# A graph-attention layer's softmax sums: half of head 0's in every fourth tile to GpSimd, transfers and copies in other places

## The chip, the cores and the metric

The kernel runs on one core of a Trainium2 chip. A core has five engines that run side by side, each with its own queue of instructions in a fixed order: TensorE (PE in the profile; PEld is its weight loads) multiplies matrices, VectorE (DVE) and ScalarE (ACT) work elementwise, GpSimd (POOL) does so more slowly and also issues DMA transfers, and SyncE (SP) issues transfers. Engines wait for one another by semaphores. The metric is the device time of one execution in microseconds (us); the time before is 2834.48 us, the median of three runs (2832.46 to 2835.08).

## The reference, cut to what matters

The model has two layers over a graph of 4096 nodes with 512 features. Layer 0 is a masked dot-product attention; the change doesn't touch it. Layer 1 is a graph attention with 8 heads of 64 columns:

```python
h = relu(layernorm(x))
data1 = (h @ W.T + b).reshape(N, H, D)              # N 4096, H 8, D 64
src = einsum('nhd,xhd->nh', data1, src_proj)        # one number per node and head
trg = einsum('nhd,xhd->nh', data1, trg_proj)
e = src.T[:, :, None] + trg.T[:, None, :]           # (head, n, m)
e = where(e >= 0, e, 0.01 * e)
e = e + adj[None, :, :]                             # added to the logit, not a mask
out = einsum('hnm,hmd->hnd', softmax(e, axis=-1), data1.transpose(1, 0, 2))
x = x + out.transpose(1, 0, 2).reshape(N, H * D)
```

For every head there are 4096 x 4096 weights, of which each output needs a weighted sum over m and the plain sum of the weights (the softmax's denominator).

## The kernel before, in words

Layer 1 works in *groups* (`groups`): 4 blocks of 1024 output nodes n (`WL`) by 2 halves of 4 heads (`HG`), so 8 groups, and in each group over 32 *tiles* of 128 neighbours m (`NT`). A step is one tile of one group. The weights of a tile lie with m on the partitions and n along the row, 128 x 1024 in fp32, one tile `pr0` to `pr3` for each head.

The exponential of the leaky logit is a product of row and column factors. ScalarE computes `ex`, the exponential of the adjacency tile (`exps`, line 1071, into PSUM, a single buffer), and `e3`, the same with a column factor (`last_exps`, line 1081, into SBUF). VectorE makes each head's weights in one instruction (`weigh`): max of a row factor `z` and a column factor, times `ex` (line 1122, heads 1 and 2) or times `e3` (line 1122, head 3, whose inputs both lie in SBUF); head 0 takes its maximum from a relu on ScalarE (`relus`, line 1104, tile `rl`, two buffers) and only subtracts and multiplies (line 1119). The order on VectorE is heads 3, 0, 1, 2. In the eight tiles of `BY_LOG` (3, 7, ..., 31) head 0's weights come from ScalarE instead: a relu `lg` of a row `u` (`logs`, line 1087), to which GpSimd adds the adjacency in two halves (`add_logs`, line 1093), and an exponential into `pr0` (line 1101). `pr0` has three buffers, `pr1` to `pr3` have two.

TensorE (`gather`) multiplies the tile's 128 neighbours' values by the weights: 16 matmuls of 32 columns by 512 (line 1157), which run four at a time in four column strips of the array, into the accumulators `pv` in PSUM. The denominators are accumulated in the bank `dn`. For heads 1 and 2 a further matmul per half row does it (line 1162). Head 3's weights are summed over the tiles on GpSimd (`acc3`, line 1133, 128 x 1024). Head 0's are summed by transfers: GpSimd issues a DMA that adds `pr0` to one of two accumulators in SBUF, in turn (line 1140), in the 24 tiles of `BY_DMA`, and TensorE sums the other eight (6, 10, 14, 18, 22, 26, 29, 31) with a column of ones, in whichever half of the strips is named by `side`. At a group's last tile TensorE adds the accumulators themselves.

The schedule is by hand. In step s the list `stages` calls each function for a tile some steps ahead: adjacency load 4 (SP), `exps` and `weigh` 1, `factors` (`e3` and relu) 2, `logs` 4, `gather` 0. Each engine gets its instructions in this order; so in step 9 VectorE makes tile 10 and GpSimd sums it, while TensorE multiplies tile 9. At a group's last tile four copies on ScalarE (line 1190) free `pv`; the copy of `dn` (line 1196) stands in the next step, behind the next relu. The group's results are finished during the next group (`finish`), one piece in each of the 15 steps of `PARTS`: transposes on TensorE, four scalings on ScalarE (line 1243) in two steps in a row, and behind the second a transfer on GpSimd that adds the layer's input to the output block `o` (line 1248, in steps 5, 9, 13 and 17); SP stores `o` three steps later (line 1246), the last one in step 18 (line 1251). In groups 0 and 1 ScalarE also scales two value blocks per tile (line 1067).

Of the kernel before, what the change touches and what calls it, by code (L numbers as in the profile page):

```python
# [8 lines left out]
FP = mybir.dt.float32  # L9
AF = mybir.ActivationFunctionType  # L10
ALU = mybir.AluOpType
# [4 lines left out]
P = 128  # L16
# [12 lines left out]
def kernel(  # L29
# [57 lines left out]
    ones = big.tile([P, 1], FP, name="ones")  # L87
# [5 lines left out]
    rl = s_n.rearrange("p h t -> p (h t)").rearrange("p (t b) -> p t b", b=NB)  # L93
# [9 lines left out]
    with tc.tile_pool(name="w0", bufs=1) as wp, tc.tile_pool(name="a0", bufs=2) as ap_, tc.tile_pool(  # L103
        name="a0s", bufs=8
# [259 lines left out]
        for b in range(1, NB):  # L364
            n = 0
# [120 lines left out]
    with tc.tile_pool(name="mx", bufs=1) as mxp, tc.tile_pool(name="b_a", bufs=6) as adjp, tc.tile_pool(  # L486
        name="b_m", bufs=4
    ) as mkp, tc.tile_pool(name="b_s", bufs=2) as sp, tc.tile_pool(
        name="b_p", bufs=6, space=PSUM
# [53 lines left out]
        early = {}  # L543
# [35 lines left out]
        for n in range(-5, len(items)):  # L579
# [3 lines left out]
            if n >= 0:  # L583
                i, j, t = items[n]
# [10 lines left out]
                if n in more:  # L595
                    f, m = more[n]
# [7 lines left out]
    with tc.tile_pool(name="c_e", bufs=4) as etp, tc.tile_pool(name="c_a", bufs=4) as adjp, tc.tile_pool(  # L604
        name="c_d", bufs=2
    ) as wkp, tc.tile_pool(name="c_m", bufs=1) as mxp, tc.tile_pool(name="c_o", bufs=4) as iop, tc.tile_pool(
        name="c_s", bufs=2
# [9 lines left out]
        src, aj, ex, mbs = {}, {}, {}, {}  # L617
# [104 lines left out]
        left, scale, norms, zs = [], {}, iter(()), {}  # L722
# [177 lines left out]
        for s in range(-5, end):  # L900
            n, q = divmod(s, NQ)
# [50 lines left out]
    va = sup.rearrange("p t (h d) -> p t h d", h=H)  # L952
# [30 lines left out]

    PARTS = (0, 1, 2, 4, 5, 6, 8, 9, 10, 12, 13, 14, 16, 17, 18)
    BY_LOG = (3, 7, 11, 15, 19, 23, 27, 31)
    BY_DMA = [m for m in range(NT) if m not in (6, 10, 14, 18, 22, 26, 29, 31)]
    after = mybir.DependencyInfo(mybir.DependencyClass.Sync, mybir.DependencyReason.DATA)

    with tc.tile_pool(name="p", bufs=2) as prp, tc.tile_pool(name="rl", bufs=2) as rlp, tc.tile_pool(
        name="io1", bufs=2
    ) as iop, tc.tile_pool(name="s1", bufs=1) as sp, tc.tile_pool(name="za", bufs=1) as zp0, tc.tile_pool(name="e3", bufs=2) as e3p, tc.tile_pool(
        name="zb", bufs=1
# [86 lines left out]
            nc.scalar.activation(x_, ra[i, m], AF.Exp, bias=ld_m[:, h // HG, m:m + 1])  # L1081
            e3[i, m] = x_

        def logs(i, m):
            if m in BY_LOG:
                r = rlp.tile([P, WL], FP, name="lg", bufs=1)
                nc.scalar.activation(r, us[i], AF.Relu, bias=nlg_m[:, groups[i][1], m:m + 1], scale=-(1.0 - SLOPE))
                rl[i, m] = r

        def add_logs(i, m, half, behind=None):  # L1090
            if m in BY_LOG:
# [15 lines left out]
        def weigh(i, m, order=ORDER):  # L1107
            h = groups[i][1] * HG
            x_ = ex.pop((i, m))
            for k in order:  # L1110
                if (i, m, k) in pr:
                    continue
                w = prp.tile([P, WL], FP, name=f"pr{k}", bufs=3 if k == 0 else 2)
                if k == 0 and (i, m) == (0, 0):
                    r = rlp.tile([P, WL], FP, name="rl")
                    nc.vector.tensor_scalar(r, zs_[0, 0], g_m[:, 0, 0:1], d_m[:, 0, 0:1], ALU.max, ALU.mult)
                    nc.vector.tensor_tensor(w, r, x_, ALU.mult)
                elif k == 0:
                    nc.vector.scalar_tensor_tensor(w, rl.pop((i, m)), ngd_m[:, h // HG, m:m + 1], x_,  # L1119
                                                   op0=ALU.subtract, op1=ALU.mult)  # L1120
                else:
                    p_ = nc.vector.scalar_tensor_tensor(w, zs_[i, k], g_m[:, h + k, m:m + 1],  # L1122
                                                        e3.pop((i, m)) if k == 3 else x_,
                                                        op0=ALU.max, op1=ALU.mult)
                    if k == 3:
                        add_logs(i, m + 1, 1, p_)
                pr[i, m, k] = w
            w = pr[i, m, 3]
            if m == 1:
                acc[i, 3] = acp.tile([P, WL], FP, name="acc3", bufs=1)  # L1130
                nc.gpsimd.tensor_tensor(acc[i, 3], pr[i, 0, 3], w, ALU.add)
            elif m > 1:
                nc.gpsimd.tensor_tensor(acc[i, 3], acc[i, 3], w, ALU.add)  # L1133
            add_logs(i, m + 2, 0)
            if m == 1:
                for n in range(2):
                    acc[i, 0, n] = acp.tile([P, WL], FP, name=f"acc0{n}", bufs=1)
                    nc.gpsimd.dma_start(acc[i, 0, n], pr[i, n, 0])
            elif m > 1 and m in BY_DMA:
                nc.gpsimd.dma_start(acc[i, 0, (len(BY_DMA) + BY_DMA.index(m)) % 2], pr[i, m, 0], accum_op=ALU.add)  # L1140

        def gather(i, m):
            b, g = groups[i]
            last = m == NT - 1
            if m == 0:
                pv[i] = ([[p_v.tile([P, BL], FP, name=f"pv{c}{q}") for q in range(HV)] for c in range(2)],
                         p_v.tile([P, BL], FP, name="dn"))
            v, dn = pv[i]
            by_pe = [u for u in range(NT) if u not in BY_DMA]
            side = sum(u < m for u in by_pe) % 2  # L1150

            def values(c):
                for q in range(HV):
                    for r in (side, 1 - side):
                        k = ((3, 0), (1, 2))[c][r]
                        for c0 in range(0, D, Q):
                            nc.tensor.matmul(v[c][q][r * D + c0:r * D + c0 + Q, :],  # L1157
                                             va[:, m, g * HG + k, c0:c0 + Q],
                                             pr[i, m, k][:, q * BL:(q + 1) * BL], start=(m == 0), stop=last)

            def den(r, w, src, q, **fl):
                nc.tensor.matmul(dn[r * Q:r * Q + w.shape[1], :], w, src[:, q * BL:(q + 1) * BL], **fl)  # L1162

            values(0)
            if last:
                for r, a in enumerate((acc[i, 0, 0], acc[i, 3])):
                    for q in range(HV):
                        den(r * HV + q, zo[:, 1:3], a, q, start=False, stop=False)
                if m in by_pe:
                    for q in range(HV):  # L1170
                        den(side * HV + q, zo[:, 1 - side:3], pr[i, m, 0], q, start=False, stop=False)
            values(1)
            for r in (side, 1 - side):
                for q in range(HV):
                    hk = g * 2 + r
                    den(r * HV + q, d0_m[:, hk, m, :] if m else d0_0[:, hk, :], pr[i, m, r + 1], q,
                        start=(m == 0), stop=(last and r == 1))
            if m in by_pe and not last:
                for q in range(HV):
                    den(side * HV + q, zo[:, 1 - side:3], pr[i, m, 0], q, start=False, stop=False)  # L1180
            if last:
                for q in range(HV):
                    den(q, zo[:, 1:3], acc[i, 0, 1], q, start=False, stop=True)
            for k in range(HG):
                pr.pop((i, m - 1, k), None)
            if last:
                os_ = [[osp.tile([P, BL], FP, name=f"os{c}{q}") for q in range(HV)] for c in range(2)]
                for c in range(2):
                    for q in range(HV):
                        nc.scalar.copy(os_[c][q], v[c][q])  # L1190
                late[i] = os_, dn

        def denominators(i):
            os_, dn = late.pop(i)
            od = osp.tile([P, BL], FP, name="od")
            nc.scalar.copy(od, dn)
            yield os_
# [56 lines left out]
        def finish_last(i):  # L1254

            ys = [ep.tile([P, WT // 2, HG, D], FP, name="e") for _ in range(2)]
            for n in range(2):
                nc.sync.dma_start(ys[n], part(x1, i, n * WT // 2, WT // 2))
            yield
            dens = denominators(i)  # L1260
            os_ = next(dens)
            pts = []
# [67 lines left out]
        weigh(0, 0, (3, 1, 2, 0))  # L1330
        scale(0, 0)
        factors(0, 1)
        logs(0, 3)
        scale(0, 1)

        stages = ((load, 4), (exps, 1), (weigh, 1), (factors, 2), (logs, 4), (scale, 2), (gather, 0))
        for s in range(len(steps)):
            for f, ahead in stages:
                if s + ahead < len(steps):
# [47 lines left out]
```

## Time and profile before

| | |
|---|---|
| profiled execution | 2832.0 us (span 2829.9) |
| median of three runs | 2834.48 us |
| TensorE busy | 2760.9 us, 98% of the span |
| VectorE busy | 2506.6 us, 89% |
| ScalarE, GpSimd busy | 1474.1 us (52%), 1395.4 us (49%) |
| layer 1, groups 1 to 7 | about 148 us each: VectorE 144 to 148, TensorE 147 to 149, GpSimd 117 to 121 |
| granted TensorE clock | 0.991 over the execution |

A line of a group of instructions names the source line, the engine, the operation, the tile written and the tiles read, the shape, the count, then the busy time in us and the mean of one in ns, then the engine's idle time just before these instructions and what ended it. A line of the timeline has the start and length in us, and in brackets the idle time before. Instructions of one engine overlap a little: the next may start shortly before the recorded end of the one before.

### The profile page before, as it was taken

Reading aid. Unit: us, or ns where it says so; the run is one execution under the profiler, and the core shown is the slowest. Engines: PE = TensorE matmul, PEld = TensorE weight load, DVE = VectorE, ACT = ScalarE, POOL = GpSimd, SP = SyncE. Lnnn points to the kernel's source line nnn. Section 1 sums busy time; section 2 is a strip of 40 time slices with the busy share of each in tenths; the row PEclk is TensorE's granted clock in tenths of the full one; section 3 lists DMA queues with packets and bytes.
Section 4 is the critical chain, followed back from the end, with each engine's and each line's share of the span. In section 5 each row is a group of like instructions: output and inputs, shape, how many; then the busy total and the mean of one; then the engine's idle time right before and its main releaser. Section 6 shows DMA issues by size and latency. Waiting matters only on the chain. (4 is left out here: it accounts for less than half of the span.)

```text
span 2829.9 us, 46835 instructions
## 1 busy us (share of the span) xinstructions
PE 2760.9 (98%) x16843; PEld 1488.1 (53%) x16843; DVE 2506.6 (89%) x3425; ACT 1474.1 (52%) x2217; POOL 1395.4 (49%) x1182
## 2 busy tenths in 40 slices
PE   7999999999999999999999799999999999999998
PEld 4885444445888888888885323323222322232222
DVE  7877799898987788888886699999999999999998
ACT  2212233333133333433432188988788878888786
POOL 5323434444010010011106687887878787878786
PEclk9999999999999999999999999999999999999999
DMA  5536898887899999998866379999999898989896
GB/s 173 175 103 254 274 338 294 298 292 268 185 188 213 194 222 256 226 219 238 221 194 158 109 195 240 241 213 249 218 246 222 239 223 237 227 242 218 211 224 168
DMA packets 535992, 629.86 MB, mean 223 GB/s; under 512 B 292152, under 2 KB 346456, under 8 KB 535760
## 3 DMA queue, kind: packets, MB, share of 16 engines
q1 hardware_dynamic: 461920, 415.87, 49.2%
q0 software_dynamic: 71824, 207.07, 33.5%
q10 hardware_dynamic: 2016, 3.93, 0.4%
q8 instruction: 132, 2.16, 0.3%
q14 instruction: 100, 0.82, 0.1%
HBM read 404.23 MB, written 107.15 MB: 181 GB/s over the span
## 5 line engine op out<-in xcount | busy, mean ns | idle before, releaser
L1157 PE MATMUL pv<-pr,sup 128*32 128x512 f32 x8192 | 986.6, 594 | 18.0 <-POOL sup L1065 14.9
L1133 POOL TENSOR_TENSOR acc<-acc,pr 128x1024 f32<-128x1024 f32 x240 | 575.0, 2396 | 149.6 <-DVE pr L1122 148.0
L1122 DVE SCALAR_TENSOR_TENSOR pr<-z,g_m,ex 128x1024 f32<-128x1024 f32 x512 | 630.4, 1270 | 4.4 <-ACT ex L1071 2.6
L1157 PEld LDWEIGHTS pv<-pr,sup 128*32 128x32 f32 x8192 | 280.2, 110 | 618.9 <-issue 563.8
L525 PE MATMUL pe<-he_t,he_t 128*128 128x512 f32 x896 | 387.9, 594 | 0.0
L679 ACT ACTIVATE d<-d 128x1024 f32<-128x1024 f32 x126 | 133.1, 1056 | 441.4 <-DVE d L671 216.9
L1122 DVE SCALAR_TENSOR_TENSOR pr<-z,g_m,e 128x1024 f32<-128x1024 f32 x256 | 343.8, 1343 | 3.4 <-PE pv L1157 3.2
L1071 ACT ACTIVATE ex<-e 128x1024 f32<-128x1024 f32 x256 | 263.2, 1028 | 144.7 <-DVE pr L1122 142.9
L1162 PE MATMUL dn<-pr,d_m 128*2 128x512 f32 x1984 | 318.1, 592 | 0.0
L1081 ACT ACTIVATE e<-e,ld_m 128x1024 f32<-128x1024 f32 x256 | 290.8, 1136 | 0.0
L525 PEld LDWEIGHTS pe<-he_t,he_t 128*128 128x128 f32 x896 | 169.9, 191 | 209.3 <-issue 193.7
L717 PE MATMUL po<-sup,u 128*128 128x256 f32 x1024 | 263.7, 380 | 0.0
L717 PE MATMUL po<-he_t,at 128*128 128x256 f32 x1024 | 262.9, 379 | 0.0
L717 PE MATMUL po<-sup,at 128*128 128x256 f32 x1024 | 245.1, 382 | 8.9 <-DVE at L688 7.7
L1119 DVE SCALAR_TENSOR_TENSOR pr<-rl,ngd_m,ex 128x1024 f32<-128x1024 f32 x191 | 242.6, 1270 | 8.4 <-ACT ex L1071 8.4
L1104 ACT ACTIVATE rl<-z,ngd_m,d_m 128x1024 f32<-128x1024 f32 x191 | 234.7, 1229 | 0.0
L804 POOL DMA_DIRECT2D he_t<-he_t x56 | 48.8, 949 | 356.5 <-ACT he_t L720 302.1
L688 DVE TENSOR_TENSOR at<-d,a 128x1024 f32<-128x1024 f32 x126 | 154.1, 1223 | 71.7 <-PE po L717 47.0
L717 PEld LDWEIGHTS po<-sup,at 128*128 128x128 f32 x1024 | 194.9, 191 | 39.0 <-DVE at L688 11.5
L717 PEld LDWEIGHTS po<-he_t,at 128*128 128x128 f32 x1024 | 194.5, 190 | 26.7 <-issue 0.3
L717 PEld LDWEIGHTS po<-sup,u 128*128 128x128 f32 x1024 | 194.4, 190 | 26.3
L530 POOL DMA_DIRECT2D er_d<-mk x136 | 74.5, 548 | 239.1 <-DVE rm L527 226.7
(271 smaller groups left out, 3830.8 us busy)
## 6 DMA issues: line engine op xcount, KB each, us to landing
e<-in_adj_t_dram SPq DMA_DIRECT2D x256, 512.0 KB, 5.9
acc<-pr POOLq DMA_DIRECT2D x192, 512.0 KB, 6.1
a<-in_adj_t_dram SPq DMA_DIRECT2D x126, 512.0 KB, 5.3
ac<-in_adj_t_dram SPq DMA_DIRECT2D x124, 256.0 KB, 5.2
ar<-in_adj_dram SPq DMA_DIRECT2D x120, 256.0 KB, 4.8
ec_d<-mc POOLq DMA_DIRECT2D x120, 256.0 KB, 4.9
er_d<-mk POOLq DMA_DIRECT2D x112, 256.0 KB, 4.6
et<-er_d SPq DMA_DIRECT2D x448, 64.0 KB, 4.1
```

Source lines behind the costliest of these rows:

```text
L525: nc.tensor.matmul(pe[:, :w], he_t[i][:, k, (t % TB) * P:(t % TB + 1) * P], he_t[j][:, k, BL - w:], start=(k == 0), stop=(k == KC - 1))
L679: nc.scalar.activation(d, d, AF.Exp)
L688: nc.vector.tensor_tensor(w, d, aj.pop((n, q)), ALU.mult)
L717: nc.tensor.matmul(acc[:, j, :], A[:, j * P:(j + 1) * P], B, start=(first_ and j == 0), stop=last, skip_group_check=True)
L1071: nc.scalar.activation(x_, ra.pop((i, m)), AF.Exp)
L1081: nc.scalar.activation(x_, ra[i, m], AF.Exp, bias=ld_m[:, h // HG, m:m + 1])
L1104: nc.scalar.activation(r, zs_[i, 0], AF.Relu, bias=ngd_m[:, h // HG, m:m + 1], scale=d_m[:, h, m:m + 1])
L1119: nc.vector.scalar_tensor_tensor(w, rl.pop((i, m)), ngd_m[:, h // HG, m:m + 1], x_, op0=ALU.subtract, op1=ALU.mult)
L1122: p_ = nc.vector.scalar_tensor_tensor(w, zs_[i, k], g_m[:, h + k, m:m + 1], e3.pop((i, m)) if k == 3 else x_, op0=ALU.max, op1=ALU.mult)
L1133: nc.gpsimd.tensor_tensor(acc[i, 3], acc[i, 3], w, ALU.add)
L1157: nc.tensor.matmul(v[c][q][r * D + c0:r * D + c0 + Q, :], va[:, m, g * HG + k, c0:c0 + Q], pr[i, m, k][:, q * BL:(q + 1) * BL], start=(m = ...
L1162: nc.tensor.matmul(dn[r * Q:r * Q + w.shape[1], :], w, src[:, q * BL:(q + 1) * BL], **fl)
```

## The change

- Head 0's sums: the tiles without a transfer are now 4, 8, ..., 28 (`BY_HALF`) and 31. In each of the seven, GpSimd copies or adds one half row (512 columns) of `pr0` into a new accumulator `acc02`, the halves taking turns, and TensorE sums the other half with one matmul; at the last tile TensorE sums `pr0` of tile 31 and `acc02`. The 24 transfers are those of all other tiles, so tiles 6, 10, 14, 18, 22, 26 and 29 have one now.
- The strips in `gather` start at one of four places, by the number of half matmuls so far, in place of one of two.
- At a group's end only the first two copies of `pv` stand behind the last tile. The other two, and the copy of `dn`, come behind the next group's exponential of tile 1 (`rest`, `copy_rest`).
- The log relu of tile 3 is made one step earlier (`early_logs`, 5 ahead), so in step 30 of the group before, in which VectorE makes tile 31.
- The relu's tile `rl` has one buffer in place of two.
- The last piece of `finish`, the last store, moves from step 18 to 21.

```diff
-    PARTS = (0, 1, 2, 4, 5, 6, 8, 9, 10, 12, 13, 14, 16, 17, 18)
+    PARTS = (0, 1, 2, 4, 5, 6, 8, 9, 10, 12, 13, 14, 16, 17, 21)
     BY_LOG = (3, 7, 11, 15, 19, 23, 27, 31)
-    BY_DMA = [m for m in range(NT) if m not in (6, 10, 14, 18, 22, 26, 29, 31)]
+    BY_HALF = (4, 8, 12, 16, 20, 24, 28)
+    BY_DMA = [m for m in range(NT - 1) if m not in BY_HALF]
...
-    with tc.tile_pool(name="p", bufs=2) as prp, tc.tile_pool(name="rl", bufs=2) as rlp, tc.tile_pool(
+    with tc.tile_pool(name="p", bufs=2) as prp, tc.tile_pool(name="rl", bufs=1) as rlp, tc.tile_pool(
...
-        def logs(i, m):
-            if m in BY_LOG:
+        def logs(i, m, early=False):
+            if m in BY_LOG and early == (m == BY_LOG[0]):
                 r = rlp.tile([P, WL], FP, name="lg", bufs=1)
                 nc.scalar.activation(r, us[i], AF.Relu, bias=nlg_m[:, groups[i][1], m:m + 1], scale=-(1.0 - SLOPE))
                 rl[i, m] = r
+
+        def early_logs(i, m):
+            logs(i, m, True)
...
             elif m > 1 and m in BY_DMA:
                 nc.gpsimd.dma_start(acc[i, 0, (len(BY_DMA) + BY_DMA.index(m)) % 2], pr[i, m, 0], accum_op=ALU.add)
+            if m in BY_HALF:
+                n = BY_HALF.index(m)
+                if n == 0:
+                    acc[i, 0, 2] = acp.tile([P, WL], FP, name="acc02", bufs=1)
+                a, w = (t[:, (1 - n % 2) * BL:(2 - n % 2) * BL] for t in (acc[i, 0, 2], pr[i, m, 0]))
+                if n < 2:
+                    nc.gpsimd.tensor_copy(a, w)
+                else:
+                    nc.gpsimd.tensor_tensor(a, a, w, ALU.add)
...
-            by_pe = [u for u in range(NT) if u not in BY_DMA]
-            side = sum(u < m for u in by_pe) % 2
+            n = sum(u < m for u in BY_HALF) % 4
+            cols = [(n + c) % 4 for c in range(4)]
...
             values(0)
             if last:
-                for r, a in enumerate((acc[i, 0, 0], acc[i, 3])):
-                    for q in range(HV):
-                        den(r * HV + q, zo[:, 1:3], a, q, start=False, stop=False)
-                if m in by_pe:
-                    for q in range(HV):
-                        den(side * HV + q, zo[:, 1 - side:3], pr[i, m, 0], q, start=False, stop=False)
+                for q in range(HV):
+                    den(q, zo[:, 1:3], acc[i, 0, 0], q, start=False, stop=False)
+                for q in range(HV):
+                    den(HV + q, zo[:, 1:3], acc[i, 3], q, start=False, stop=False)
+                for q in range(HV):
+                    ones(0, pr[i, m, 0], q)
+                for q in range(HV):
+                    ones(1, acc[i, 0, 2], q)
             values(1)
...
-            if m in by_pe and not last:
-                for q in range(HV):
-                    den(side * HV + q, zo[:, 1 - side:3], pr[i, m, 0], q, start=False, stop=False)
+            if m in BY_HALF:
+                ones(n // 2, pr[i, m, 0], n % 2)
...
                 os_ = [[osp.tile([P, BL], FP, name=f"os{c}{q}") for q in range(HV)] for c in range(2)]
-                for c in range(2):
-                    for q in range(HV):
-                        nc.scalar.copy(os_[c][q], v[c][q])
-                late[i] = os_, dn
-
-        def denominators(i):
-            os_, dn = late.pop(i)
+                for q in range(HV):
+                    nc.scalar.copy(os_[0][q], v[0][q])
+                late[i] = os_, v[1], dn
+
+        def rest(i, m):
+            if i and m == 0:
+                copy_rest(i - 1)
+
+        def copy_rest(i):
+            os_, v, dn = late[i]
+            for q in range(HV):
+                nc.scalar.copy(os_[1][q], v[q])
             od = osp.tile([P, BL], FP, name="od")
             nc.scalar.copy(od, dn)
+            late[i] = os_, od
...
-        stages = ((load, 4), (exps, 1), (weigh, 1), (factors, 2), (logs, 4), (scale, 2), (gather, 0))
+        stages = ((load, 4), (exps, 1), (rest, 0), (weigh, 1), (factors, 2), (logs, 4), (early_logs, 5), (scale, 2), (gather, 0))
```

More of the change, by code (lines that the diff above doesn't have):

```diff
@@ L1148, in gather @@
             v, dn = pv[i]
-            by_pe = [u for u in range(NT) if u not in BY_DMA]
-            side = sum(u < m for u in by_pe) % 2
+            n = sum(u < m for u in BY_HALF) % 4
+            cols = [(n + c) % 4 for c in range(4)]
             def values(c):
                 for q in range(HV):
-                    for r in (side, 1 - side):
+                    for col in cols:
+                        r, c0 = col // 2, col % 2 * Q
                         k = ((3, 0), (1, 2))[c][r]
[L1156 to L1159, printed above, removed]
+                        nc.tensor.matmul(v[c][q][col * Q:(col + 1) * Q, :],
+                                         va[:, m, g * HG + k, c0:c0 + Q],
+                                         pr[i, m, k][:, q * BL:(q + 1) * BL], start=(m == 0), stop=last)
@@ L1161, in den, with ones @@
             def den(r, w, src, q, **fl):
                 nc.tensor.matmul(dn[r * Q:r * Q + w.shape[1], :], w, src[:, q * BL:(q + 1) * BL], **fl)
+            def ones(side, src, q, stop=False):
+                den(side * HV + q, zo[:, 1 - side:3], src, q, start=False, stop=stop)
             values(0)
             if last:
-                for r, a in enumerate((acc[i, 0, 0], acc[i, 3])):
-                    for q in range(HV):
-                        den(r * HV + q, zo[:, 1:3], a, q, start=False, stop=False)
@@ L1169, in gather @@
-                if m in by_pe:
-                    for q in range(HV):
-                        den(side * HV + q, zo[:, 1 - side:3], pr[i, m, 0], q, start=False, stop=False)
-            values(1)
-            for r in (side, 1 - side):
-                for q in range(HV):
-                    hk = g * 2 + r
-                    den(r * HV + q, d0_m[:, hk, m, :] if m else d0_0[:, hk, :], pr[i, m, r + 1], q,
-                        start=(m == 0), stop=(last and r == 1))
-            if m in by_pe and not last:
-                for q in range(HV):
-                    den(side * HV + q, zo[:, 1 - side:3], pr[i, m, 0], q, start=False, stop=False)
+                for q in range(HV):
+                    den(q, zo[:, 1:3], acc[i, 0, 0], q, start=False, stop=False)
@@ new lines, in gather @@
+                for q in range(HV):
[4 more added lines that the diff above has]
+                    ones(1, acc[i, 0, 2], q)
+            values(1)
+            for col in cols:
+                r, q = divmod(col, HV)
+                hk = g * 2 + r
+                den(col, d0_m[:, hk, m, :] if m else d0_0[:, hk, :], pr[i, m, r + 1], q,
+                    start=(m == 0), stop=(last and r == 1))
@@ L1181, in gather @@
+            if m in BY_HALF:
+                ones(n // 2, pr[i, m, 0], n % 2)
             if last:
                 for q in range(HV):
-                    den(q, zo[:, 1:3], acc[i, 0, 1], q, start=False, stop=True)
+                    ones(0, acc[i, 0, 1], q, True)
             for k in range(HG):
@@ L1187, in gather, with denominators @@
                 os_ = [[osp.tile([P, BL], FP, name=f"os{c}{q}") for q in range(HV)] for c in range(2)]
-                for c in range(2):
-                    for q in range(HV):
-                        nc.scalar.copy(os_[c][q], v[c][q])
-                late[i] = os_, dn
-        def denominators(i):
-            os_, dn = late.pop(i)
+                for q in range(HV):
[8 more added lines that the diff above has]
+                nc.scalar.copy(os_[1][q], v[q])
             od = osp.tile([P, BL], FP, name="od")
             nc.scalar.copy(od, dn)
+            late[i] = os_, od
+        def denominators(i):
+            os_, od = late.pop(i)
             yield os_
@@ L1259, in finish_last @@
             yield
+            copy_rest(i)
             dens = denominators(i)
@@ L1332 @@
         factors(0, 1)
-        logs(0, 3)
+        early_logs(0, 3)
         scale(0, 1)
-        stages = ((load, 4), (exps, 1), (weigh, 1), (factors, 2), (logs, 4), (scale, 2), (gather, 0))
+        stages = ((load, 4), (exps, 1), (rest, 0), (weigh, 1), (factors, 2), (logs, 4), (early_logs, 5), (scale, 2), (gather, 0))
         for s in range(len(steps)):
```

## The prediction

> The text numbers things so: a *group* is 1024 output rows by 4 heads (eight groups, 0 to 7), a *tile* m (0 to 31) is 128 neighbours of a group, and the *weight product of head k* is VectorE's instruction that makes pr[k].
>
> **What bounds the kernel now.** I read the page for where the time lies, then the table by stage, the groups of instructions, and the engines' own timelines inside single groups. Layer 1 runs from 1627 to 2819 us in eight nearly equal groups. The table by stage, one group (span, then busy time of TensorE, its weight loads, VectorE, ScalarE, GpSimd):
>
> ```profile
> 2371.00:2519.00 148.00, 146.82 (x1348) 43.68 (x1344) 145.81 (x123) 121.19 (x143) 117.29 (x75) 1.00 0.93 233
> ```
>
> TensorE and VectorE are both within 2% of the span, so a change pays only if it leaves VectorE alone. The groups for layer 1:
>
> ```profile
> L1122 DVE SCALAR_TENSOR_TENSOR pr<-z,g_m,e 128x1024 f32<-128x1024 f32 x256 | 343.8, 1343 | 3.4 <-PE pv L1157 3.2
> L1119 DVE SCALAR_TENSOR_TENSOR pr<-rl,ngd_m,ex 128x1024 f32<-128x1024 f32 x191 | 242.6, 1270 | 8.4 <-ACT ex L1071 8.4
> L1093 POOL TENSOR_TENSOR lg<-lg,e 128x512 f32<-128x512 f32 x128 | 164.5, 1285 | 38.5 <-DVE pr L1122 35.2 <-DMA e<-in_adj_t_dram 3.2
> L1140 POOL DMA_DIRECT2D acc<-pr x176 | 153.3, 871 | 1.6 <-DMA acc<-pr 0.8 <-issue 0.7
> L1248 POOL DMA_DIRECT2D o<-x x28 | 34.0, 1213 | 3.9 <-ACT o L1243 1.7 <-DVE pr L1122 1.6 <-issue 0.6
> ```
>
> Products follow each other 1.20 us apart, so a plain tile takes VectorE 4.77 us, a tile of BY_LOG (three products) 3.61; TensorE takes 4.29 for either. VectorE's idle time is tiny, and the first row has a mean of 1343 ns against 1270: head 3's product, alone in reading both inputs from SBUF, is stretched. GpSimd's and VectorE's timelines around tiles 10 to 12 of group 5 show by what (start, length, idle before):
>
> ```profile
> 2419.03 2.38 POOL L1133 TENSOR_TENSOR acc<-acc,pr 128x1024 f32<-128x1024 f32 x1
> 2421.36 1.22 POOL L1248 DMA_DIRECT2D o<-x  x1
> 2422.64 2.39 POOL L1133 TENSOR_TENSOR acc<-acc,pr 128x1024 f32<-128x1024 f32 x1
> ...
> 2424.80 1.32 DVE L1122 SCALAR_TENSOR_TENSOR pr<-z,g_m,e 128x1024 f32<-128x1024 f32 x1
> 2426.04 1.27 DVE L1119 SCALAR_TENSOR_TENSOR pr<-rl,ngd_m,ex 128x1024 f32<-128x1024 f32 x1
> ```
>
> GpSimd sums tile 10, issues the transfer of an output block (o), sums tile 11, and is done at 2425.03, 0.23 us after head 3's product of tile 12 began. Here it just fits. The same place in group 1, where o came 0.42 us later:
>
> ```profile
> 1809.74 1.23 POOL L1248 DMA_DIRECT2D o<-x  x1 [0.42 <-ACT o L1243]
> 1810.56 2.82 POOL L1133 TENSOR_TENSOR acc<-acc,pr 128x1024 f32<-128x1024 f32 x1
> ...
> 1812.79 1.68 DVE L1122 SCALAR_TENSOR_TENSOR pr<-z,g_m,e 128x1024 f32<-128x1024 f32 x1
> 1814.40 1.27 DVE L1119 SCALAR_TENSOR_TENSOR pr<-rl,ngd_m,ex 128x1024 f32<-128x1024 f32 x1
> ```
>
> In both the product ends 1.09 us after GpSimd's sum, and the next product starts 1.01 to 1.02 after it, not 1.20 after its own start: an overlap of d costs VectorE d - 0.19. At d = 0.23 that is 0.04, at 0.59 it is 0.40; one for one.
>
> **The change, part by part.** On each engine the instructions stand in the order in which the stages write them.
>
> *Transfers moved to tiles 6, 10, 14, 18.* Their number is the same (24 a group), but tiles 4, 8, ..., 28 lose theirs and 6, 10, 14, 18, 22, 26 and 29 gain one. In groups 1 to 7 the four o transfers are issued right behind the work of tiles 6, 10, 14, 18, which issued none until now. So between "sum of tile 10" and "o" stands one more transfer of 0.85 to 0.87 us, and the sum of tile 11 ends that much later: d grows from 0.23 to 1.09. VectorE pays 0.90 in place of 0.04, so +0.86, four times a group. The bounds are 0.58 (a transfer in a pair at the start of a group, 579 ns) and 0.90. In groups 2 to 7: 24 x 0.86 = 20.6. In group 1 the transfer fills the 0.42 that GpSimd waited anyway: 4 x 0.44 = 1.8. Group 0 has no o. **+22.4 us** (16 to 23).
>
> The Trainium skill states the rule behind this: a VectorE instruction with two SBUF inputs and a GpSimd instruction that reads SBUF need one lock, and the loser blocks fully (SBUF — State Buffer, "Who interferes with whom"). The rows agree, but charge the overlap less 0.19. By the rule to the letter the next part would be 40 x 0.28 = 11 in place of 4, and the time some 7 us more; the measurement decides.
>
> *Half sums on GpSimd.* Tiles 4, 8, ..., 28 add a copy (first two) or a 128x512 sum, 1285 ns by L1093's row, behind the tile's own sum. That is exactly where a log addition already stands in tiles 5, 9, ...: it overlaps the next head 3 product by some 0.29, and that product takes 1.37 in place of 1.27, with the next one 1.30 behind it, not 1.20. So 5 sums x 8 groups x 0.10 = 4.0, and 16 copies, whose length no row of this shape shows: between 0 (short enough to end before the product) and 0.10 each. I take the middle. **+4.8 us** (4.0 to 5.6).
>
> *TensorE's load.* A matmul fills one of four strips for 0.86 us; a group costs its fullest strip. Before, strips 0 and 1 carry 160 + 4 (half of eight tiles) + 2 at the end = 166 slots; after, 160 + 2 + 3 = 165: some 7 us in all. It pays only where VectorE waits for TensorE to free a product buffer:
>
> ```profile
> 2429.96 1.29 DVE L1122 SCALAR_TENSOR_TENSOR pr<-z,g_m,e 128x1024 f32<-128x1024 f32 x1 [0.28 <-PE pv L1157]
> ```
>
> Such waits, at tiles 12 to 19, make 1.2 to 1.4 us in groups 2, 3, 5, 6 and 7; group 4 has 1.85 at the same tiles, by a late ScalarE. With VectorE 3.4 later through these tiles and TensorE 0.4 to 0.9 earlier they vanish: **-8.4 us**. The rest of TensorE's saving is worth nothing, since VectorE is late.
>
> *Last store moved from step 18 to 21.* At step 18 SP waits for the o transfer just issued, and the adjacency loads stand behind it:
>
> ```profile
> 2463.01 0.40 SPq L1251 DMA_DIRECT2D out_dram<-o  x1
> ...
> 2471.79 1.52 DVE L1122 SCALAR_TENSOR_TENSOR pr<-z,g_m,e 128x1024 f32<-128x1024 f32 x1
> ...
> 2475.74 1.16 ACT L1101 ACTIVATE pr<-lg,t_m 128x1024 f32<-128x1024 f32 x1 [1.73 <-DMA acc<-pr]
> ```
>
> Late loads make tile 22's product long (1.52 to 2.24 us in groups 1 to 7); the exponential of tile 23 waits for tile 20's transfer, which no longer exists. Against the usual 4.87 and 3.61 these two tiles lose 6.2 us over all groups. At step 21 that o has landed three steps before, so SP passes at once. **-6.2 us.**
>
> *The group change.* VectorE now waits once there, because four copies and the log relu stand ahead of an exponential:
>
> ```profile
> 2075.62 1.13 ACT L1087 ACTIVATE lg<-u,nlg_m 128x1024 f32<-128x1024 f32 x1
> 2076.66 2.02 ACT L1190 COPY os<-pv 128x512 f32<-128x512 f32 x4
> 2078.55 1.05 ACT L1071 ACTIVATE ex<-e 128x1024 f32<-128x1024 f32 x1
> ...
> 2079.64 1.28 DVE L1119 SCALAR_TENSOR_TENSOR pr<-rl,ngd_m,ex 128x1024 f32<-128x1024 f32 x1 [1.17 <-ACT ex L1071]
> ...
> 2086.73 1.15 ACT L1101 ACTIVATE pr<-lg,t_m 128x1024 f32<-128x1024 f32 x1 [1.30 <-DMA acc<-pr]
> ```
>
> That goes: 7 x 1.26 = -8.8. But two waits come. First, the relu moves into the step in which VectorE makes tile 31, where VectorE needs only 3.61 us and ScalarE then has 0.96 + 1.04 + 1.14 + 1.04 = 4.18 of work: the exponential of tile 0 is 0.57 late, less 0.1 of play: +0.48. Second, the exponential of tile 3 waits for tile 0's transfer, issued 4.98 us after head 3's product of tile 1 starts and landing 2.9 to 4.8 later. VectorE's stall after that product hid this; without it the chain 4.98 + 4.1 + 0.2 + 1.06 + 1.06 = 11.4 us stands against VectorE's 10.74: +0.7 (0 to 1.4). So 7 x (0.48 + 0.7 - 1.26) = **-0.5 us** (-5.5 to +4.4). TensorE's 1.1 us wait for the last copy vanishes too, to no gain.
>
> *One buffer for the relu in place of two.* It must now wait for head 0's product of the tile before: 0.4 us later on ScalarE. In groups 2 to 7 that is covered: in the fullest step ScalarE is done 0.2 us before its next exponential may begin. In groups 0 and 1 two scalings (0.57) stand behind it and that slack is gone: about 0.15 in 13 steps, **+2.0 us** (0 to 4).
>
> *End.* TensorE ends 6.3 us after VectorE's last product, 5.4 if it is not behind: **-0.9 us**.
>
> Sum: 22.4 + 4.8 - 8.4 - 6.2 - 0.5 + 2.0 - 0.9 = +13.2. The profiled execution took 2832.0, the median of three is 2834.5; the same step from that gives 2847.7, and I say 2847.
>
> **The rivals.**
> 1. *GpSimd's lateness is hidden* (other side). If the sum of tiles 7, 11, 15, 19 does not come later by a transfer, or head 3's product is not held, the 22.4 fall away and 2834.5 + 13.2 - 22.4 = 2825 remains, faster. It decides from a price under 0.25 us at each of the 28 places. For it: GpSimd is busy 79% only. Against it: group 1's rows, and that the order puts both transfers in front of that sum. Chance 0.15.
> 2. *The group change pays.* If tile 0's transfer lands as in its fastest group (2.9), the second wait is nil and the sum is 5 us lower, 2842; with the 0.58 price for a transfer besides (24 x 0.28 less) it is 2835, no change. For it: group 7's landing. Against it: the other six take 3.9 to 4.8. Chance 0.12.
> 3. *GpSimd waits for landings.* Transfers alternate between two accumulators, each waiting for the one before on it; those of tiles 5 and 7, ..., 21 and 23 are now neighbours on one, 8.4 us apart, where landings take 5.5 to 8.6 now, up to 11 at tile 20. One wait of 1.5 us a group passes on to VectorE: +12, 2859. Chance 0.10.
> My forecast has 0.63.
>
> **How the numbers follow.** About 0.2% (5.7 us) is what can be told from no change. Forecast and rival 3 are slower, 0.73 together, less 0.04 for the forecast's low edge (0.58 a transfer, 2840): slower 0.69, same 0.16, faster 0.15. All terms at their low ends together give 2834, all at their high ends 2856; the one profiled execution lies 2.5 from the median, so I take 2833 to 2858, which holds rival 2. Rival 1 and the rest of rival 3 stay outside, under 0.2.
>
> **What would show it.** Right: head 3's products of tiles 8, 12, 16, 20 at some 2.2 us in groups 1 to 7, no VectorE wait on TensorE, tile 22's product at 1.38, a VectorE wait before head 0's product of tile 0 and another at tile 3, TensorE with idle time inside groups. Wrong: those four products still at 1.32, or new idle time on GpSimd ended by a landing.

## The result, and the profile after

The changed kernel takes 2847.36 us (median of five runs, 2845.70 to 2850.36) against 2833.23 for the kernel before in the same comparison: ratio 1.0050, 95% interval 1.0039 to 1.0062. It is 14 us slower; 2847 was forecast.

The table by stage for one group of the changed kernel (columns as before):

```profile
2380.00:2530.00 150.00, 148.78 (x1338) 44.78 (x1334) 147.98 (x122) 121.68 (x141) 124.57 (x83) 1.00 0.92 228
```

The two windows, of 148 and 150 us, are cut a little loosely: by the starts of head 3's products this group takes 150.5 us, where it took 147.4. Both busy engines fill it as before; of itself this says nothing about the cause. The groups of instructions do, since head 3's product, 1343 ns before, has grown and no other product has:

```profile
L1126 DVE SCALAR_TENSOR_TENSOR pr<-z,g_m,ex 128x1024 f32<-128x1024 f32 x512 | 630.2, 1270 | 6.3 <-ACT ex L1072 5.5 <-PE dn L1175 0.8
L1126 DVE SCALAR_TENSOR_TENSOR pr<-z,g_m,e 128x1024 f32<-128x1024 f32 x256 | 361.8, 1413 | 0.0
```

Now the place in group 5 that the prediction showed, GpSimd's and then VectorE's timeline of the changed kernel (start, length):

```profile
2431.55 2.38 POOL L1137 TENSOR_TENSOR acc<-acc,pr 128x1024 f32<-128x1024 f32 x1
2433.88 0.84 POOL L1144 DMA_DIRECT2D acc<-pr  x1
2434.46 1.50 POOL L1274 DMA_DIRECT2D o<-x  x1
2435.20 3.14 POOL L1137 TENSOR_TENSOR acc<-acc,pr 128x1024 f32<-128x1024 f32 x1
...
2437.32 2.12 DVE L1126 SCALAR_TENSOR_TENSOR pr<-z,g_m,e 128x1024 f32<-128x1024 f32 x1
2439.36 1.27 DVE L1123 SCALAR_TENSOR_TENSOR pr<-rl,ngd_m,ex 128x1024 f32<-128x1024 f32 x1
```

Between the sum of tile 10 and the transfer of o there is now tile 10's own transfer, so the sum of tile 11 ends at 2438.34, 1.02 us after head 3's product of tile 12 began, where it was 0.23. The product takes 2.12 us in place of 1.32 and ends 1.10 us after the sum.

At the group change (ScalarE and VectorE) the two waits that were to come are there, at tile 0 and at tile 3, and the one at tile 1 is gone:

```profile
2379.64 1.13 ACT L1088 ACTIVATE lg<-u,nlg_m 128x1024 f32<-128x1024 f32 x1
2380.68 1.01 ACT L1072 ACTIVATE ex<-e 128x1024 f32<-128x1024 f32 x1
2395.78 1.15 ACT L1105 ACTIVATE pr<-lg,t_m 128x1024 f32<-128x1024 f32 x1 [3.49 <-PE pt L1226]
...
2381.72 1.28 DVE L1123 SCALAR_TENSOR_TENSOR pr<-rl,ngd_m,ex 128x1024 f32<-128x1024 f32 x1 [0.38 <-ACT ex L1072]
2397.87 2.47 DVE L1126 SCALAR_TENSOR_TENSOR pr<-z,g_m,ex 128x1024 f32<-128x1024 f32 x2 [1.64 <-ACT ex L1072]
```

(TensorE, named beside the wait of 3.49 us, is not what ended it: tile 0's transfer landed at 2395.60, 0.18 us before.)

Tile 22's product, in which the moved store shows, takes 1.37 us in place of 1.52 in this group:

```profile
2480.91 1.37 DVE L1126 SCALAR_TENSOR_TENSOR pr<-z,g_m,e 128x1024 f32<-128x1024 f32 x1
```

To read all groups at once, take the distance between the starts of successive head 3 products, less 4.77 us (3.61 in the tiles of BY_LOG), and add it up over the eight groups. The distance that begins with tile m's product counts as tile m's. This is all that VectorE loses in layer 1 against that pace:

| VectorE's loss, us | before | after | difference |
|---|---|---|---|
| tiles 8, 12, 16, 20 | 8.1 | 23.0 | +14.9 |
| tiles 7, 11, 15, 19 | 4.1 | 1.8 | -2.4 |
| tiles 5, 9, 13, 17, 21, 25, 29 | 1.0 | 6.8 | +5.7 |
| tiles 22 and 23 | 7.0 | 0.5 | -6.5 |
| tiles 0 to 3 | 13.8 | 15.9 | +2.2 |
| the others | 5.1 | 4.5 | -0.6 |
| together | 39.1 | 52.4 | +13.3 |

In these two executions the rest of the span differs by 2.6 us ahead of layer 1, where no instruction was changed, and by -0.2 from head 3's last product to the end.

### The profile page after: what moved, and what is told of

The parts are those of the page before. It is cut to its first block, busy times and chain, and to the rows that moved or that the text cites. A ratio compares the mean times of both kernels' runs of the same rounds, so it can differ in the third digit from the quotient of the medians.

```text
span 2845.6 us, 46629 instructions
## 1 busy us (share of the span) xinstructions
PE 2769.5 (97%) x16763; PEld 1507.6 (53%) x16763; DVE 2522.8 (89%) x3425; ACT 1485.3 (52%) x2217; POOL 1456.4 (51%) x1238
## 5 line engine op out<-in xcount | busy, mean ns | idle before, releaser
L1170 PE MATMUL pv<-pr,sup 128*32 128x512 f32 x8192 | 1046.3, 594 | 22.4 <-POOL sup L1066 14.9
L1137 POOL TENSOR_TENSOR acc<-acc,pr 128x1024 f32<-128x1024 f32 x240 | 595.5, 2481 | 115.2 <-DVE pr L1126 115.2
L1170 PEld LDWEIGHTS pv<-pr,sup 128*32 128x32 f32 x8192 | 306.8, 110 | 615.0 <-issue 514.7
L1175 PE MATMUL dn<-pr,d_m 128*2 128x512 f32 x1984 | 365.1, 592 | 0.0
L1126 DVE SCALAR_TENSOR_TENSOR pr<-z,g_m,e 128x1024 f32<-128x1024 f32 x256 | 361.8, 1413 | 0.0
L688 DVE TENSOR_TENSOR at<-d,a 128x1024 f32<-128x1024 f32 x126 | 154.0, 1223 | 66.1 <-PE po L717 46.8
```

The costliest lines, as they stand in the source:

```text
L688: nc.vector.tensor_tensor(w, d, aj.pop((n, q)), ALU.mult)
L1170: nc.tensor.matmul(v[c][q][col * Q:(col + 1) * Q, :], va[:, m, g * HG + k, c0:c0 + Q], pr[i, m, k][:, q * BL:(q + 1) * BL], start=(m == 0) ...
```

## The experiments

Three theories stood at the start. A, the prediction's: the transfer that now stands in front of the o transfer delays GpSimd's next sum, and this holds head 3's product. B: the half sums, the single relu buffer and the group change cost the time, and the transfers are hidden. C: the transfers' traffic costs it, not their place. In the comparisons below the kernel before took 2829.38 to 2831.05 us, not 2833.23, so runs are compared by their ratios to it.

**Four transfers a group taken away**

```diff
-            elif m > 1 and m in BY_DMA:
+            elif m > 1 and m in BY_DMA and m not in (6, 10, 14, 18):
```

> The changed kernel without head 0's transfers of tiles 6, 10, 14 and 18 (their weights are missing from head 0's denominator). Theory A, the transfer in front of the output block's transfer delays the next sum on GpSimd, which holds head 3's product: the products of tiles 8, 12, 16, 20 fall from 2.05-2.15 us to 1.3, VectorE saves 0.8 us at 24 places and 0.4 at four (21 us), some 3 us of which come back as waits on TensorE: about 2829. Theory B, the half sums, the single relu buffer and the group change cost the time and the transfers are hidden: within 3 us of the changed kernel's 2847.

Measured: 2828.14 us, ratio to the kernel before 0.9999 (0.9990 to 1.0007), so 14 us under the changed kernel by the ratios where 18 were expected. The products fall to 1.28 to 1.33 us at tile 12 of groups 2 to 7, the loss at tiles 8, 12, 16 and 20 from 23.0 to 6.3 us, and 2.6 of that comes back at tiles 7, 11, 15 and 19, mostly as waits on TensorE. VectorE there, at the tile shown above:

```profile
2425.03 1.32 DVE L1126 SCALAR_TENSOR_TENSOR pr<-z,g_m,e 128x1024 f32<-128x1024 f32 x1
```

Theory B falls. In group 1, where o waits for ScalarE's scalings in the kernel before, the transfer fills that wait and costs less, as the prediction has it: at tiles 12, 16 and 20 the loss, 0.78 to 0.80 us each, falls to 0.40 to 0.43, which is what the kernel before has there. Tile 12 of group 1 in the changed kernel and in this one:

```profile
1836.22 2.05 DVE L1126 SCALAR_TENSOR_TENSOR pr<-z,g_m,e 128x1024 f32<-128x1024 f32 x1
...
1834.49 1.68 DVE L1126 SCALAR_TENSOR_TENSOR pr<-z,g_m,e 128x1024 f32<-128x1024 f32 x1
```

Only tile 8 of group 1 goes the other way (0.8, now 2.4 us): there GpSimd issued the transfer of o 2.3 us after the scaling's end, and the product took 3.68 us. What held that one issue is not shown; for this the group's sum does not fall (3.2, now 3.6).

**The same transfers, o's in another step**

```diff
-    PARTS = (0, 1, 2, 4, 5, 6, 8, 9, 10, 12, 13, 14, 16, 17, 21)
+    PARTS = (0, 1, 2, 4, 5, 6, 7, 8, 9, 10, 11, 12, 13, 14, 15, 16, 17, 18, 19, 22)
...
+                if old is not None:
+                    nc.sync.dma_start(part(out, i, t - 4, 2), old)
                 yield
+                if ready is not None:
+                    nc.gpsimd.dma_start(ready, part(x1, i, t - 2, 2), accum_op=ALU.add)
+                    old = ready
+                    yield
...
-                nc.gpsimd.dma_start(o, part(x1, i, t, 2), accum_op=ALU.add)
-                old = o
-                yield
+                ready = o
```

> The changed kernel with all its transfers, but each output block's transfer is issued two steps later (steps 7, 11, 15, 19) and its store two steps after the old place. GpSimd then has that transfer behind a half sum, and no two transfers in one step. Theory A: products of tiles 8, 12, 16, 20 back to 1.3 us, about 2829, under the kernel before. Theory C, it is the transfers' traffic, not their place on GpSimd: as the changed kernel, 2845 to 2850. Theory B: the same 2845 to 2850.

Measured: 2825.44 us, ratio 0.9986 (0.9977 to 0.9994): 18 us under the changed kernel by the ratios, and under the kernel before. GpSimd and VectorE of this kernel around tiles 11 to 13 of group 5:

```profile
2420.13 0.85 POOL L1144 DMA_DIRECT2D acc<-pr  x1
...
2423.78 1.28 POOL L1153 TENSOR_TENSOR acc<-acc,pr 128x512 f32<-128x512 f32 x1
2425.01 1.18 POOL L1269 DMA_DIRECT2D o<-x  x1
2426.30 2.39 POOL L1137 TENSOR_TENSOR acc<-acc,pr 128x1024 f32<-128x1024 f32 x1
...
2420.00 1.28 DVE L1126 SCALAR_TENSOR_TENSOR pr<-z,g_m,e 128x1024 f32<-128x1024 f32 x1
2424.77 1.38 DVE L1126 SCALAR_TENSOR_TENSOR pr<-z,g_m,e 128x1024 f32<-128x1024 f32 x1
```

The issue of tile 11's transfer, from 2420.13, runs beside head 3's product of tile 12, which takes its usual 1.28 us. Issued from 2425.01, the o transfer stands beside the product of tile 13 (2424.77 to 2426.15) and doesn't lengthen it; only the half sum before it does (1.38). The loss at tiles 8, 12, 16 and 20 is 1.7 us over all groups. Theory C falls: the traffic is the same. Theory A holds, and what decides is the place alone.

**Head 0's sums as before**

```diff
-    BY_HALF = (4, 8, 12, 16, 20, 24, 28)
-    BY_DMA = [m for m in range(NT - 1) if m not in BY_HALF]
+    BY_DMA = [m for m in range(NT) if m not in (6, 10, 14, 18, 22, 26, 29, 31)]
...
-            if m in BY_HALF:
-                ones(n // 2, pr[i, m, 0], n % 2)
+            if m in by_pe and not last:
+                for q in range(HV):
+                    den(side * HV + q, zo[:, 1 - side:3], pr[i, m, 0], q, start=False, stop=False)
```

> The changed kernel with head 0's sums as before (transfers in the old tiles, TensorE's two matmuls in eight tiles, no half sums); group change, early relu, single relu buffer and the moved store stay. Theory A and my terms: the kernel before less 6 for the store, less 0.5 for the group change, plus 2 for the single buffer: 2827 to 2831, with TensorE's waits at tiles 12 to 19 back. Theory B: at least 2840.

Measured: 2824.99 us, ratio 0.9984 (0.9976 to 0.9993): 4.4 us under the kernel before, within the 2 to 6 us expected, and 18.7 us under the changed one by the ratios. So the loss lies in the sums' part of the change, and the rest of the change is a gain. Here and in the run before this, the undisturbed groups are bound by TensorE, which has no idle time in them, and they are equally long from TensorE's first matmul to the next group's: 147.35 and 147.30 us. So the new sums save TensorE 0.05 us a group, not 0.86. TensorE's timeline at tile 1 shows where it went, first with the old sums, then with the new:

```profile
2378.62 3.64 PE L1160 MATMUL pv<-pr,sup 128*32 128x512 f32 x32
2383.05 1.06 PE L1212 MATMUL pt<-pick,od 128*128 128x8 f32 x8
2384.04 3.64 PE L1160 MATMUL pv<-pr,sup 128*32 128x512 f32 x32
```

```profile
2373.64 0.60 PE L1170 MATMUL pv<-pr,sup 128*32 128x512 f32 x2
2378.85 1.06 PE L1226 MATMUL pt<-pick,od 128*128 128x8 f32 x8
2379.84 3.64 PE L1170 MATMUL pv<-pr,sup 128*32 128x512 f32 x32
```

Tile 1 lasts 5.42 us from its first matmul to the next tile's with the old sums and 6.20 with the new. The matmuls for the denominators' turn (pt) and the transposes take all four strips. My reading is that strips that are out of step, because one or two of them had a matmul more, must come level first, so a round (one matmul's time in all four strips) is lost whether one strip was filled or four. Both kinds of sums lose one at the transposes of tiles 6, 10 and 14: tile 6 lasts 5.84 us with two strips filled (old) and 5.82 with one (new), where tile 2, with transposes and no such matmul, lasts 5.02. The old ones then need four rounds more, the new ones three (one for tiles 16 to 28, two at the end) and one at tile 1 for the last accumulator's half row.

**The store alone**

```diff
-    PARTS = (0, 1, 2, 4, 5, 6, 8, 9, 10, 12, 13, 14, 16, 17, 18)
+    PARTS = (0, 1, 2, 4, 5, 6, 8, 9, 10, 12, 13, 14, 16, 17, 21)
```

> The kernel before with only the last store moved from step 18 to 21. My term: head 3's product of tile 22 falls from 1.5-2.2 us to 1.4 and the wait of tile 23 for late loads goes: 6 us less, 2827. Rival: the wait is passed on to tile 23's exponential, which still waits for tile 20's transfer, and 1 to 2 us of it remain: 2829. If the store hides anyway: 2833.

Measured: 2825.97 us, ratio 0.9986 (0.9977 to 0.9994), 3.4 to 4.0 us less where 6 were expected. The loss at tiles 22 and 23 goes from 7.0 to 1.2 us, so my term is right at its place, and the passed-on wait didn't show. Tiles 0 to 3 gave 1.6 us back in this execution.

**Two relu buffers again, beside the old sums**

```diff
-    with tc.tile_pool(name="p", bufs=2) as prp, tc.tile_pool(name="rl", bufs=1) as rlp, tc.tile_pool(
+    with tc.tile_pool(name="p", bufs=2) as prp, tc.tile_pool(name="rl", bufs=2) as rlp, tc.tile_pool(
```

> The run with the old sums, but the relu has its two buffers again, so it is the kernel before with the group change and the moved store. If the single buffer costs what the trace of the old-sums run shows in groups 0 and 1 (2.2 us at tile 1 of group 0, less 1.0 at tile 3; 0.24 us behind each tile 5, 9, ..., 29): 2820 to 2822 where the old-sums run has 2825. If those waits were there anyway: 2825.

Measured: 2823.09 us, ratio 0.9972 (0.9962 to 0.9983), against 0.9984 with one buffer: 3.4 us less, with intervals that overlap. The profile settles the place. Group 0's loss falls from 6.3 to 4.1 us and that of tiles 5, 9, ..., 29 of groups 0 and 1 from 3.8 to 0.01. In the changed kernel the first wait of ScalarE, and VectorE's behind it, read so:

```profile
1635.20 1.24 ACT L1108 ACTIVATE rl<-z,ngd_m,d_m 128x1024 f32<-128x1024 f32 x1 [3.37 <-DVE pr L1121]
...
1638.43 1.28 DVE L1123 SCALAR_TENSOR_TENSOR pr<-rl,ngd_m,ex 128x1024 f32<-128x1024 f32 x1 [2.13 <-ACT ex L1072]
```

In group 0 head 0's product is the last of tile 0's four, not the second, so the relu of tile 1 stands behind all of them, and the exponential of tile 1 behind it.

**Tile 0's transfer early**

```diff
-                for n in range(2):
-                    acc[i, 0, n] = acp.tile([P, WL], FP, name=f"acc0{n}", bufs=1)
-                    nc.gpsimd.dma_start(acc[i, 0, n], pr[i, n, 0])
+                for n in range(i > 0, 2):
+                    start_sum(i, n)
...
+        def first_sum(i, m):
+            if i and m == 0:
+                start_sum(i, 0)
...
-        stages = ((load, 4), (exps, 1), (rest, 0), (weigh, 1), (factors, 2), (logs, 4), (early_logs, 5), (scale, 2), (gather, 0))
+        stages = ((load, 4), (exps, 1), (rest, 0), (weigh, 1), (factors, 2), (logs, 4), (early_logs, 5), (scale, 2), (gather, 0), (first_sum, 1))
```

> The changed kernel with the transfer of tile 0's weights issued at the end of the step before instead of behind tile 1's sum. My chain for the wait at tile 3 (transfer issued 4.98 us after head 3's product of tile 1, landing 4 us later, exponential of tile 3 behind it): VectorE's loss at tile 3, 8.4 us over the groups in the changed kernel, falls to 2 (the reciprocal): 6 us less than the changed kernel, so about 8 over the kernel before (ratio 1.003). Rival: the exponential then waits for GpSimd's log addition, and at most 2 us are saved (1.0045).

Measured: 2838.20 us, ratio 1.0023 (1.0013 to 1.0033), where the changed kernel has 1.0050. The loss at tile 3 falls from 8.4 to 2.4 us, as the chain has it. Part of it returns: the loss at tiles 7, 11, 15 and 19 grows from 1.8 to 3.8 us, with waits on TensorE.

**No half sums on GpSimd**

```diff
-                if n < 2:
-                    nc.gpsimd.tensor_copy(a, w)
-                else:
-                    nc.gpsimd.tensor_tensor(a, a, w, ALU.add)
```

> The changed kernel without GpSimd's copies and half sums (half of head 0's weights in tiles 4, 8, ..., 28 are missing from its denominator). Lock priced by the rows: 0.10 us at the products of tiles 13, 17, 21, 25, 29 of each group and nothing behind the two copies: 4 us less than the changed kernel (ratio to the kernel before 1.0035). By the letter of the full lock, 0.28 each: 11 us less (1.001). Theory B: the whole loss of 14 us goes (1.000).

(A tile of zeros stands in for the accumulator of the half sums, and TensorE still adds it.)

Measured: 2838.55 us, ratio 1.0026 (1.0017 to 1.0035), the interval of which just holds the 1.0035. The profile is plainer. In groups 2 to 7 the tiles behind half sums lose 0.01 us a group instead of 0.5, which is 0.10 each, and nothing stood behind the two copies in either kernel. By the full lock's letter it would have been 1.4 a group. In groups 0 and 1 nothing changes at these tiles (2.0 and 1.7 us with the half sums and without): there the single relu buffer sets the pace. A further 2.4 us of the difference lies at tile 3, in how early tile 0's transfer landed in each execution; I don't count that as the half sums'.

**One version from the readings, in three steps.** All three are the kernel before with the group change, the moved store, two relu buffers, o's transfers two steps later, tile 0's transfer early and the early relu in step 29. They differ in the tiles that TensorE sums:

```diff
-    BY_DMA = [m for m in range(NT) if m not in (6, 10, 14, 18, 22, 26, 29, 31)]
+    BY_DMA = [m for m in range(NT) if m not in (4, 6, 8, 10, 12, 14, 31)]
...
-        stages = ((load, 4), (exps, 1), (weigh, 1), (factors, 2), (logs, 4), (scale, 2), (gather, 0))
+        stages = ((load, 4), (exps, 1), (rest, 0), (weigh, 1), (factors, 2), (logs, 4), (early_logs, 6), (scale, 2), (gather, 0), (first_sum, 1))
```

> What the readings point to, in one kernel: the kernel before with the group change, the moved store and two relu buffers; the output blocks' transfers two steps later as in the run before; tile 0's transfer early; the early relu one step earlier still (step 29); and TensorE's sums of head 0 in pairs of tiles between two transposes (4, 6, 8, 10, 12, 14) and tile 31, 25 transfers. If half-filled strips cost a whole round at each transpose, TensorE's group falls from 147.35 to 145.6 us and VectorE's to 145: 2808 to 2812. If TensorE's time follows the number of matmuls alone: 2818. If transfers in sixteen tiles in a row (15 to 30) make GpSimd wait for landings: 2822 or more.

Measured: 2825.91 us, ratio 0.9980 (0.9971 to 0.9988), not the hoped-for 2808 to 2812 but in the range that was to tell of waits for landings. Head 3's products of one group after another are 145.70 us apart at best (group 3), mostly 147.9 to 149.5, and 154.0 in group 0. I took the 145.70 for TensorE's time, but TensorE's own shortest group is 146.49 (from tile 2 to the next group's tile 2), one round less than 147.35 and not two: each pair fills one round (tile 6 lasts 5.84 us with all four strips filled), but at the group's end tile 31 lies on the same two strips as both of head 0's accumulators, which makes three rounds there. The wait at tile 0 is gone (0.0 to 0.05 us). ScalarE's exponentials wait 18.6 us for landings. I took this for the effect of sixteen transfers in a row, and added a pair of tiles for TensorE:

```diff
-    BY_DMA = [m for m in range(NT) if m not in (4, 6, 8, 10, 12, 14, 31)]
+    BY_DMA = [m for m in range(NT) if m not in (4, 6, 8, 10, 12, 14, 20, 24, 31)]
```

> The one version with tiles 20 and 24 summed on TensorE as well, a further pair, so 23 transfers and none in the tiles whose buffer the exponential of tiles 23 and 27 takes over. If its lost time was exponentials that waited for late landings behind sixteen transfers in a row (18.6 us on ScalarE): the groups come to 146.6 us, one round over its undisturbed 145.70, and the kernel to 2814 to 2819. If the time was lost elsewhere: 2823 to 2826 as it was.

Measured: 2826.20 us, ratio 0.9987 (0.9978 to 0.9996): a miss. The late landings are nearly gone (3.1 us), but TensorE's groups are back at 147.35 us: the forecast of 146.6 added a round to VectorE's 145.70, where TensorE's 146.49 and a round are 147.35. In groups 2 to 6 TensorE has no idle time, so this bounds them. VectorE's distance at tile 4, up to 6.9 us, shows a second fault, and GpSimd's timeline its source:

```profile
2374.91 0.57 POOL L1146 DMA_DIRECT2D acc<-pr  x1
...
2382.39 0.88 POOL L1142 DMA_DIRECT2D acc<-pr  x1 [2.62 <-DVE pr L1125]
```

The transfers alternate between two accumulators, and the expression that picks one counts from the end. With an odd number of transfers those of tiles 1 and 2 fall on the same one, and the second waits for the first to land. The version with 25 transfers has this wait too (1.3 to 2.5 us in four groups). In the groups that TensorE bounds it cost nothing. And nine tiles leave tile 31's half on the strips that the last accumulator's half takes too, a round more. Hence the third, with eight tiles:

```diff
-    BY_DMA = [m for m in range(NT) if m not in (4, 6, 8, 10, 12, 14, 20, 24, 31)]
+    BY_DMA = [m for m in range(NT) if m not in (4, 6, 8, 10, 12, 14, 24, 31)]
```

> The one version with eight tiles on TensorE again (4, 6, 8, 10, 12, 14, 24 and 31), so 24 transfers. With an odd number the transfers of tiles 1 and 2 fall on one accumulator, and GpSimd waited 2.6 us there for a landing; with 24 they alternate. TensorE has one round less than with nine tiles: tile 24's half and tile 31's lie on different strips. If these two explain the loss of the last two versions: groups at 146.5 us, no long period at tile 4, 2816 to 2820, the best of the runs. If landings behind the transfers of tiles 15 to 23 hold the exponentials: 2823 to 2826 again.

Measured: 2821.37 us, ratio 0.9966 (0.9955 to 0.9977), the lowest of all and under both kernels, 0.8% under the changed one. Its interval overlaps that of the kernel before with only the group change and the moved store (0.9972), so what the rest of it adds is not shown by the time. VectorE's tile 4 takes 4.68 us in groups 1 to 7 again, four groups of VectorE are at 146.0 to 146.3 us, and TensorE's shortest take 146.49, the 146.5 expected. What remains above the hoped-for 2816 to 2820 lies in part at tiles 22 and 23 (5.8 us). In group 0 an exponential waits 4.4 us there for a landing. In groups 3, 5 and 7 it is theory A's mechanism again: in group 3 tile 20's transfer waits 1.17 us, until tile 18's on the same accumulator has landed, o's transfer stands behind it, and head 3's product of tile 22 takes 2.29 us.

## Why the prediction was right, point by point

The time, the sign and the mechanism came out as put; several of the terms did not. That the terms' sum, +13.2, meets the +13.3 of the table and the -0.2 behind it to 0.1 us is luck: the measured parts differ from the terms by -1.4 (transfers and TensorE's waits), -1.1 (half sums and buffer), -0.3 (store), +2.7 (tiles 0 to 3), +0.7 (end) and -0.6 (the other tiles), which cancel.

- **Transfers moved (+22.4).** Right. In groups 2 to 7 the products of tiles 8, 12, 16 and 20 took 2.1 us mostly and lost 0.84 to 0.88 us each, 0.80 to 0.84 more than the 0.04 to 0.05 before (0.86 forecast), where VectorE had not waited for TensorE; taking four transfers away brought the kernel to the time before. In group 1 each of the four lost 0.78 to 0.80 us against 0.41 to 0.43 before, 0.37 to 0.39 more where 0.44 was forecast.
- **TensorE's waits (-8.4).** Waits on TensorE fall from 4.8 to 0.8 us by VectorE's idle time (each loses some 0.07 us more, since products that don't wait overlap by that). They didn't vanish: in groups 2 and 7, where tile 0's transfer landed early and VectorE lost nothing at tile 3 but the reciprocal, tiles 7 and 11 still lost 0.5 to 0.7 us together. This term and the first were to bring 14.0 us; tiles 7, 8, 11, 12, 15, 16, 19 and 20 brought 12.6.
- **TensorE's load (some 7 us saved, worth nothing).** The step that failed is the count of 166 and 165 slots in the fullest strip. It let strips run out of step for a whole group, where full-width matmuls stand at five tiles (1, 2, 6, 10 and 14). Runs with the old and the new sums both bound by TensorE differ by 0.05 us a group. The error cost the forecast nothing, because VectorE was the later engine.
- **Half sums (+4.8) and the single buffer (+2.0).** 6.8 together, 5.7 in the table, by errors that cancel. The half sums are 0.10 us each as read from the log additions, with nothing for the copies, but only in groups 2 to 7: 3.0 us. The single buffer was mis-sized: tiles 5, 9, ..., 29 of groups 0 and 1 lost 3.8 us where I had 2.0, and in groups 0 and 1 this hid the half sums. A further 2.2 us at tile 1 of group 0, offset by 1.0 at tile 3, was not in my sum at all, since I took the product's place in tile 0 to be the usual one.
- **Last store (-6.2).** -6.5, and -5.8 with the store alone.
- **Group change (-0.5).** Tile 0: +0.48 in each of seven groups, as forecast. Tile 1: the 1.26 is gone. Tile 3: 0.0 to 2.5 us, 0.9 on average where I had 0.7, as the transfer lands 2.9 to 6.2 us after its issue. With group 0's 1.2 the whole change at tiles 0 to 3 is +2.2. That this wait hangs on the transfer is shown by the run with the early transfer.
- **End (-0.9).** -0.2.
- **The rivals.** The first (lateness hidden) is ruled out. The third (GpSimd waits for landings) comes to 2.8 us of GpSimd's time in two waits in the changed kernel, not 12 of VectorE's; the version with 23 transfers shows such waits in six groups (1.1 to 2.6 us each).

**The rule of the Trainium skill.** SBUF — State Buffer, "Who interferes with whom", says that a VectorE instruction with two SBUF inputs contends with a GpSimd instruction that reads SBUF, by an exclusive lock. That the lock is held for the whole instruction it says of VectorE's two-port modes; read for this case too, that is the full lock. The traces agree in kind: head 3 products that began 0.19 us or more before the end of a GpSimd sum or log addition ended some 1.08 us behind it (median 1.085 us over 161 such products before, 1.084 over 210 after; one, in group 0 before, took 1.26), and the two transfers shown above, issued under such a product, did not lengthen it. They differ from the plain letter in size: by the recorded starts and ends 0.19 us of the overlap is free. Whether the lock is let go before GpSimd's recorded end is not shown.

## What to carry to other kernels

Where two engines hold each other up, as head 3's product and GpSimd's sums do here, an engine that is idle a fifth of the time can still set the pace: look not at its busy share but at whether its next sum begins before the other engine's product does, and put transfers into the place where they run beside that product. A term read from a row of the same shape and place (0.10 us behind a log addition, 0.40 us at an overlap of 0.59) carried over within a tenth; the terms that were counted from the code without a row, the strips and the first tile, did not. And a wait removed in front of a fixed chain, here a transfer's landing, is worth only what that chain leaves.

## What was not expected of the hardware

- Ahead of full-width transposes a round of the four column strips cost the same however full it was: tile 6 lasts 5.82 us with one strip filled, 5.84 with two, 5.84 with four, and tile 2, with none, 5.02.
- A transfer behind two others lands late. Those of tiles 7, 11, 15 and 19, issued 3 to 4 us behind two transfers, landed 9.2 to 10.7 us after issue in groups 1 to 7, against 4.9 to 8.9 before and 6.4 to 9.1 with o's transfers two steps later. Nothing waited for them there.
- The landing of one and the same transfer, tile 0's, varied from 2.9 to 6.2 us between the groups of one execution, and VectorE's loss at tile 3 with it, from 0 to 2.5 us beyond the reciprocal.
